# Experts summed in one TensorE bank, and attention divided on channel partitions

## The chip, the cores and the metric

The kernel runs on one core of one Trainium2 chip. The metric is the device time of one execution in microseconds. A profile records one such execution: what each engine did and when, what it waited for, and every DMA.

## The reference

The input is `x`, float32, 4 images of 128 channels and 64 x 64 pixels. Two layers follow each other, everything in float32.

```python
# layer 0
x = x + conv_mamba(group_norm(x))
# layer 1, on tokens t = (4, 4096, 128)
t = t + attention(ln(t))        # 4 heads of 32, softmax over 4096 keys
t = t + moe(ln(t))              # 8 experts, the best 2 of each token
# moe:
probs = softmax(x @ router_w + router_b)
top_p, top_i = top_k(probs, 2)
top_p = top_p / top_p.sum(-1)
expert_out = einsum("bnd,edc->bnec", x, expert_w) + expert_b
return einsum("bnk,bnkc->bnc", top_p, gathered(expert_out, top_i))
```

`conv_mamba` is a depthwise 3 x 3 convolution with norms and a GELU, then a state-space scan: the 128 channels form 4 groups of 32, which the same weights expand to 64 inner channels each, with 16 states for each inner channel, a recurrence over all 4096 pixels, and a gated output projection.

## The kernel before

**Blocks and units.** An image is cut into 8 blocks of 512 pixels. A block of the scan is 2 halves (`p`) of 16 states (`n`), so there are 4 x 8 x 2 x 16 = 1,024 units (b, i, p, n). The main loop issues one unit in each slot. `queued` ties every instruction of an engine to the one before it, so that each engine runs in the order in which the loop issues; DMAs, on SP's queue, are among them. Nearly all instructions are recorded by this one helper, which is why the profile gives line L445 to them; they are told apart by the names of their tiles.

**One slot.** (1) `flush` issues the stores that `send` has collected. (2) `fetched` asks for the `rows` (512 KB, B and C rows of the scan spread over 128 partitions) of the unit three slots ahead. `until` must first see that this unit's `inputs` task is done; while it is not, `until` makes catch-up passes, which advance the two lanes and do nothing else. (3) `decayed` computes `da` for the next unit (ScalarE Exp). (4) An attention group: 4 score matmuls `sc`, 2 Exps `pT` of 128 x 1024. (5) `scan`: VectorE multiplies `h<-rows,du`, scans, and multiplies `hc<-rows,h`. (6) TensorE adds `hc` into the bank `y` with an identity matmul; for images after the first, GpSimd first adds each pair of `hc`, which halves these matmuls. (7) The 4 `av` matmuls of the attention group of the slot before (`weighted`). The lanes advance at fixed places between these.

**Lanes.** Two queues of tasks, X and Y, each written as a generator that yields between stages; a lane advances two stages in a slot. Each lane has one PSUM bank (`work("X")`, `work("Y")`) and four rotating SBUF tiles (`tmp`). Y takes group norms, `first_norm`, `conv` and `inputs` (which also uses bank X for two short matmuls); X takes `closed` (end of layer 0 for a block: output projection `wout`, norms, q, k, v), `divided` and `finished` (the rest of layer 1 for a block). After the last unit both lanes take `finished`.

**Attention.** Keys are taken in 4 parts of 1,024, queries in 4 parts, 4 heads. `weighted` leaves a head's sums and its softmax denominator in `avs`, channels on partitions, and stores them to DRAM. `divided` reads the 4 heads back (`avl`), turns them with TensorE, and multiplies by the reciprocal on VectorE into `ao`, tokens on partitions. `finished` turns `ao` back into `aT`, applies the output projection, normalises and routes.

**Experts.** For each of 4 tiles of 128 tokens and each half of the experts, one matmul (two passes of TensorE, as each full float32 matmul here) computes 4 experts for 128 tokens into the lane's bank, and then VectorE folds them one by one:

```python
vector.scalar_tensor_tensor(
    acc[:, j, :], ps[:, e, :], pr[:, j, k : k + 1], acc[:, j, :],
    ALU.mult, ALU.add,
)
```

These stages are marked `"short"`, and a lane in them may advance four stages in a slot. At the end `acc` is turned with TensorE and joined with the expert biases in one bank, copied to `res` and stored.

The general path behind `tc.If` does not run with these inputs.

Of the kernel before, what the change touches and what calls it, by code (L numbers as in the profile page):

```python
# [13 lines left out]
ALU = mybir.AluOpType  # L14
# [22 lines left out]
def conv_mamba_attn_moe_kernel(ctx: ExitStack, tc: tile.TileContext, t: dict):  # L37
# [488 lines left out]

    group_of, y0_of, xn_of, pairs_of, in_of, gated, kqv = {}, {}, {}, {}, {}, {}, {}
# [147 lines left out]
    def inputs(b, i, p):  # L675

        xn, pairs = xn_of[b, i], pairs_of[b, i]
        r = slice(DI * p, DI * p + DI)
        ps = work("Y")
# [15 lines left out]
        bc = mix.tile([DI, BLK], F32, name="bc")  # L695
# [65 lines left out]
    def closed(b, i):  # L761
# [20 lines left out]
        summed(ps, [(wout[:, p, :], gated.pop((b, i, p))) for p in range(2)])  # L782
# [29 lines left out]
        split = []  # L812
        for d, w, bias in ((kd, wkn, bkn), (qd, wqn, bqn)):
            ps = work("X")
            mm(ps, w, xa)
            yield
            full = side.tile([P, BLK], F32, name="full")
            scalar.activation(full, ps, AF.Identity, bias=bias)
            hi = side.tile([P, BLK], F32R, name="hi", bufs=2)
            scalar.activation(hi, ps, AF.Identity, bias=bias)  # L820
            yield

            split.append((d, full, hi))
            lower(split.pop(), sj)
# [9 lines left out]

    def lower(what, s):
        d, full, hi = what
        lo = side.tile([P, BLK], F32R, name="lo", bufs=2)
        vector.tensor_sub(lo, full, hi.bitcast(F32))
        for half, w in enumerate((hi, lo)):
            w = w.bitcast(F32)  # L840
            if len(d.shape) == 4:
                send(d[:, :, half, s], w[:, None, :].to_broadcast([P, 2, BLK]))
            else:
                send(d[:, half, s], w)
# [96 lines left out]
    sums, partial, ao_of = [None], {}, {}  # L941

    def weighted(group):
# [10 lines left out]
        if last:  # L954
            avs = att.tile([P, BLK], F32, name="avs", bufs=2)
            scalar.copy(avs, av)
            if prev is not None:
                gpsimd.tensor_add(avs, avs, prev)

            d = dram.tile([P, BLK], F32, name=f"avd{q}{h}")  # L960
            send(d, avs)
            partial[b, q, h] = d
            if final and h == NH - 1:
                lanes["X"].append((("div", b, q), divided(b, q), []))
                for u in range(2):
                    i = 2 * q + u
                    lanes["X"].append((
                        ("out", b, i), lambda lane, b=b, i=i: finished(b, i, lane),
                        [("div", b, q)],
                    ))  # L970

    def divided(b, q):

        ao = att.tile([P, 2, NT, NH, DH], F32, name="ao", bufs=2)
        ao_of[b, q] = ao

        def load(h):
            w = att.tile([P, BLK], F32, name="avl", bufs=2)
            sync.dma_start(out=w, in_=partial.pop((b, q, h)))
            return w  # L980

        ahead = load(0)
        yield
        yield
        for h in range(NH):
            now = ahead
            if h + 1 < NH:
                ahead = load(h + 1)
            ps = transposed("X", by_tile(now))
            yield  # L990
            ps = ps.rearrange("p (j u d) -> p u j d", u=2, d=2 * DH)
            rden = small.tile([P, 2, NT, 1], F32, name="rden")
            vector.reciprocal(rden, ps[:, :, :, DH : DH + 1])
            vector.tensor_mul(
                ao[:, :, :, h, :], ps[:, :, :, 0:DH], rden.to_broadcast([P, 2, NT, DH])
            )
            yield

    def finished(b, qb, lane):

        ao = ao_of[b, qb // 2][:, qb % 2]
        td = kqv[b][3]
        s = slice(qb * BLK, (qb + 1) * BLK)
        acc = side.tile([P, NT, C], F32, name="acc", bufs=2)
        sync.dma_start(out=acc.rearrange("p j c -> p (j c)"), in_=td[:, s])
        ps = transposed(lane, ao.rearrange("p j h d -> p j (h d)"))
        yield
        aT = tmp(lane, "aT")
        scalar.copy(aT, ps)
# [32 lines left out]
        vector.tensor_reduce(m, pr, AX.X, ALU.add)  # L1042
        vector.reciprocal(m, m)
        vector.tensor_mul(pr, pr, m.to_broadcast(wide))
# [22 lines left out]
        ewf = ew.rearrange("p e c -> p (e c)")  # L1067
        for j in range(NT):
            for u in range(2):
                ps = work(lane, [P, NE // 2, C])  # L1070
                mm(
                    ps.rearrange("p e c -> p (e c)"), xf[:, j * P : (j + 1) * P],
                    ewf[:, u * BLK : (u + 1) * BLK],
                )
                yield "short"
                for e in range(NE // 2):
                    k = NE // 2 * u + e
                    vector.scalar_tensor_tensor(
                        acc[:, j, :], ps[:, e, :], pr[:, j, k : k + 1], acc[:, j, :],
                        ALU.mult, ALU.add,  # L1080
                    )
                yield "short" if k < NE - 1 or j < NT - 1 else None
# [6 lines left out]
        scalar.copy(prT, ps[0:NE, :])  # L1089
        yield  # L1090
        ps = work(lane)
# [253 lines left out]
```

## Time and profile before

| | |
|---|---|
| Median of 3 runs | 5860.53 us (5855.43 to 5865.17) |
| Profiled execution | 5853.82 us |
| Its span, first to last instruction | 5852.1 us |
| Mean granted TensorE clock | 0.94 |
| TensorE / VectorE / ScalarE / GpSimd busy | 87% / 72% / 68% / 35% |
| DMA: bytes, mean rate | 1030 MB, 176 GB/s |

In a line of a group, the first numbers after the bar are the time in which at least one instruction of the group ran and the mean length of one in ns; after the second bar comes the idle time of the engine before them and what ended it. A line of a stretch gives for each engine its busy time and its instructions, then the granted TensorE clock, the share of the time in which the DMA engines were busy, and their rate. A line of waits gives the waiting engine and tile, what it waited for, the sum in us, the number of waits and the longest.

### The profile page before, as it was taken

Reading aid. Unit: us, or ns where it says so; the run is one execution under the profiler, and the core shown is the slowest. Engines: PE = TensorE matmul, PEld = TensorE weight load, DVE = VectorE, ACT = ScalarE, POOL = GpSimd, SP = SyncE. Lnnn points to the kernel's source line nnn. Section 1 sums busy time; section 2 is a strip of 40 time slices with the busy share of each in tenths; the row PEclk is TensorE's granted clock in tenths of the full one; section 3 lists DMA queues with packets and bytes.
Section 4 is the critical chain, followed back from the end, with each engine's and each line's share of the span. In section 5 each row is a group of like instructions: output and inputs, shape, how many; then the busy total and the mean of one; then the engine's idle time right before and its main releaser. Section 6 shows DMA issues by size and latency. Waiting matters only on the chain. (4 is left out here: it accounts for less than half of the span.)

```text
span 5852.1 us, 61426 instructions
## 1 busy us (share of the span) xinstructions
PE 5075.6 (87%) x18378; PEld 2129.7 (36%) x18378; DVE 4221.9 (72%) x7155; ACT 3988.0 (68%) x6116; POOL 2033.6 (35%) x1821
## 2 busy tenths in 40 slices
PE   4676898988989898898999998898999998998896
PEld 2222343333333333333333333333333343343332
DVE  4888766778877787787888887888888888712222
ACT  3454676877767776777777776677877777665452
POOL 2333222335423443444443443444443434310000
PEclk8777999999999998999999999999999999999997
DMA  3455565556545555556555555457555555533211
GB/s 98 167 177 169 196 203 182 190 209 223 202 149 172 198 186 197 172 198 219 185 199 199 188 199 191 155 196 252 191 192 199 183 201 185 190 134 102 99 58 35
DMA packets 405509, 1030.33 MB, mean 176 GB/s; under 512 B 42785, under 2 KB 126130, under 8 KB 405170
## 3 DMA queue, kind: packets, MB, share of 16 engines
q1 hardware_dynamic: 404002, 1025.53, 51.5%
q8 instruction: 149, 2.44, 0.2%
q14 instruction: 190, 1.56, 0.1%
q10 hardware_dynamic: 1168, 0.80, 0.1%
HBM read 875.11 MB, written 134.22 MB: 172 GB/s over the span
## 5 line engine op out<-in xcount | busy, mean ns | idle before, releaser
L445 ACT ACTIVATE pT<-sc 128x1024 f32<-128x1024 f32 x2048 | 1981.1, 1020 | 879.0 <-PE sc L445 875.5
L445 PE MATMUL av<-pT,v 128*64 128x512 f32 x8192 | 2012.4, 612 | 0.5 <-ACT avs L445 0.2
L445 DVE TENSOR_TENSOR_SCAN h<-da,state,h 128x512 f32<-128x512 f32 x896 | 1271.6, 1419 | 276.2 <-ACT da L445 191.5
L445 PE MATMUL sc<-qs,ks 128*128 128x512 f32 x4096 | 1326.7, 445 | 76.7 <-ACT pT L445 40.3
L445 POOL TENSOR_TENSOR hc<-hc 128x512 f32<-128x512 f32 x384 | 557.4, 1452 | 1541.4 <-DVE hc L445 1367.3
L445 PEld LDWEIGHTS sc<-qs,ks 128*128 128x128 f32 x4096 | 724.5, 193 | 663.0 <-issue 240.9
L445 PEld LDWEIGHTS av<-pT,v 128*64 128x64 f32 x8192 | 503.9, 138 | 1198.3 <-issue 1115.1
L445 DVE TENSOR_TENSOR hc<-rows,h 128x512 f32<-128x512 f32 x1024 | 828.2, 809 | 73.6 <-DVE h L445 2.3
L445 DVE TENSOR_TENSOR h<-rows,du 128x512 f32<-128x512 f32 x1024 | 821.7, 802 | 57.3 <-DMA rows<-bcd 30.9
L445 PE MATMUL y<-hc,ident 128*128 128x512 f32 x1280 | 734.3, 660 | 79.6 <-DVE hc L445 70.0
L445 ACT ACTIVATE da<-delta,amat 128x512 f32<-128x512 f32 x1024 | 749.7, 732 | 30.9 <-DVE h L445 28.7
L445 ACT COPY state<-h 128x1 f32<-128x1 f32 x896 | 176.8, 197 | 373.3 <-DVE h L445 373.0
L445 DVE SCALAR_TENSOR_TENSOR acc<-ps_X,prX,acc 128x128 f32<-128x128 f32 x864 | 301.8, 349 | 169.6 <-PE ps_X L445 145.3
L445 ACT ACT_TABLE_LOAD x318 | 408.0, 1283 | 20.0 <-PE ps_Y L445 15.3
L445 PE MATMUL ps_X<-w_ew,xf 128*128 128x512 f32 x432 | 257.2, 679 | 112.4 <-DVE acc L445 112.2
L445 PEld LDWEIGHTS y<-hc,ident 128*128 128x128 f32 x1280 | 248.7, 206 | 257.1 <-DVE hc L445 129.6
L445 DVE RECIPROCAL rden<-ps_X 128x8 f32<-128x8 f32 x64 | 13.0, 203 | 348.8 <-PE ps_X L445 348.6
L445 POOL TENSOR_SCALAR rsX<-mvX 128x4 f32<-128x4 f32 x92 | 48.3, 525 | 600.6 <-DVE mvX L445 593.6
L445 POOL TENSOR_SCALAR du<-e 128x512 f32<-128x512 f32 x64 | 129.3, 2020 | 322.3 <-ACT e L445 322.3
L445 POOL TENSOR_TENSOR avs<-avs,prev 128x512 f32<-128x512 f32 x64 | 94.6, 1478 | 420.4 <-ACT avs L445 345.8
L445 POOL TENSOR_SCALAR rsY<-mvY 128x4 f32<-128x4 f32 x100 | 54.9, 549 | 533.6 <-DVE mvY L445 532.0
L445 ACT ACTIVATE xt<-ps_Y,shiftY,rsY 128x128 f32<-128x128 f32 x380 | 143.5, 467 | 127.4 <-POOL shiftY L445 119.9
(244 smaller groups left out, 5052.1 us busy)
## 6 DMA issues: line engine op xcount, KB each, us to landing
rows<-bcd SPq DMA_DIRECT2D x1024, 512.0 KB, 4.9
ks<-kd SPq DMA_DIRECT2D x256, 512.0 KB, 6.3
qs<-qd SPq DMA_DIRECT2D x130, 512.0 KB, 5.6
v<-vd SPq DMA_DIRECT2D x256, 256.0 KB, 6.2
avd<-avs SPq DMA_DIRECT2D x128, 256.0 KB, 2.0
pairs<-xn SPq DMA_DIRECT2D x128, 128.5 KB, 2.4
qd<-hi SPq DMA_DIRECT2D x32, 512.0 KB, 5.6
qd<-lo SPq DMA_DIRECT2D x32, 512.0 KB, 5.9
```

The source lines that it names most:

```text
L445: return lambda *args, **kw: queued(op(*args, **kw))
```

## The change

- **Experts.** The routing weights of the 8 experts (`prT`, 8 x 512) are stored to DRAM, and each pair of rows is read back spread over all partitions (`share`, 512 KB). VectorE multiplies the normalised tokens `xf` by it, 128 x 1024 at once, and TensorE adds the products with the experts' weights, all eight, into the bank in which biases and the turned residual lie already. The softmax's own normalisation is dropped, since the two best are normalised again. The `"short"` stages go.
- **Exclusion.** Bank X is now occupied from the biases to the copy of `res`. The set `held` keeps `inputs` (which uses bank X) and this part of `finished` apart: each waits for the other, two stages at a time.
- **Division.** `weighted` stores the last sums into one DRAM tensor, sums and denominators apart. `inverted` reads the denominators 128 x 32, takes reciprocals and stores them; it is run in three steps 2, 4 and 6 slots later, outside the lanes. `finished` reads the sums as `aT`, channels on partitions, and the reciprocals spread over the channels as `inv`, and VectorE multiplies. `divided`, its turns and the copy of `aT` go.
- **Pairs.** The pairwise addition of `hc` on GpSimd starts at slot 128 (`ALONE`) instead of 256.
- **Output projection in `closed`.** Each half now writes only its 64 output partitions, instead of both adding over 128.
- **q and k.** ScalarE no longer writes `full`; VectorE takes `lo` from the bank. `bc` moves to a `tmp` tile.

```diff
@@ inputs
+        while held:
+            yield
+            yield
+        held.add("in")
...
+        held.clear()
-        bc = mix.tile([DI, BLK], F32, name="bc")
+        bc = tmp("Y", "bc")[0:DI, :]
@@ closed
-        summed(ps, [(wout[:, p, :], gated.pop((b, i, p))) for p in range(2)])
+        for p in range(2):
+            r = slice(DI * p, DI * p + DI)
+            mm(ps[r, :], wout[:, p, r], gated.pop((b, i, p)))
...
-            full = side.tile([P, BLK], F32, name="full")
-            scalar.activation(full, ps, AF.Identity, bias=bias)
...
+            vector.scalar_tensor_tensor(
+                lo, ps, bias, hi.bitcast(F32), ALU.add, ALU.subtract
+            )
@@ weighted
+            if not final:
+                partial[b, q, h] = dram.tile([P, BLK], F32, name=f"avd{q}{h}")
+                send(partial[b, q, h], avs)
+                return
+            if h == 0:
+                total[b, q] = dram.tile([2, 2, NH, DH, BLK], F32, name=f"total{q}")
+            d = total[b, q]
+            send(d[:, :, h].rearrange("u k r q -> (u k) r q"), avs)
+            if h == NH - 1:
+                work_left = inverted(b, q)
+                later.extend((slot + n, work_left) for n in (2, 4, 6))
+    def inverted(b, q):
+        den = small.tile([P, 2 * NH * BLK // P], F32, name="den", bufs=1)
+        n = den.shape[1]
+        for u in range(2):
+            sync.dma_start(
+                out=den[DI * u : DI * u + DI, :],
+                in_=total[b, q][u, 1, :, 0].rearrange("h (a n) -> h a n", n=n),
+            )
+        yield
+        vector.reciprocal(den, den)
+        inverse[b, q] = d = dram.tile([2, NH, BLK], F32, name="inverse")
+        send(d.rearrange("u h (a n) -> (u h a) n", n=n), den)
+        yield
+        for u in range(2):
+            lanes["X"].append((
+                ("out", b, 2 * q + u), lambda lane, i=2 * q + u: finished(b, i, lane), [],
+            ))
+        yield
@@ finished
-        ps = transposed(lane, ao.rearrange("p j h d -> p j (h d)"))
-        yield
-        aT = tmp(lane, "aT")
-        scalar.copy(aT, ps)
+        aT, inv = tmp(lane, "aT"), tmp(lane, "inv")
+        sync.dma_start(out=aT, in_=total[b, q][u, 0].rearrange("h d q -> (h d) q"))
+        sync.dma_start(
+            out=inv, in_=inverse[b, q][u][:, None, :].to_broadcast([NH, DH, BLK])
+        )
...
+        vector.tensor_mul(aT, aT, inv)
...
-        for j in range(NT):
-            for u in range(2):
-                ps = work(lane, [P, NE // 2, C])
-                mm(...xf[:, j * P : (j + 1) * P], ewf[:, u * BLK : (u + 1) * BLK])
-                yield "short"
-                for e in range(NE // 2):
-                    vector.scalar_tensor_tensor(...)
...
+        shares = dram.tile([NE, BLK], F32, name=f"shares{lane}")
+        send(shares, prT)
+        yield
+        while lane == "X" and held:
+            yield
+            yield
+        if lane == "X":
+            held.add("out")
+        def share(e):
+            if lane == "X":
+                w = side.tile([P, 2, BLK], F32, name="share", bufs=3)
+            else:
+                w = mix.tile([P, 2, BLK], F32, tag="rows", name="share", bufs=4)
+            sync.dma_start(
+                out=w.rearrange("p k q -> p (k q)"),
+                in_=shares[e : e + 2].rearrange("e q -> (e q)")[None].to_broadcast([P, 2 * BLK]),
+            )
+            return w
...
+        ahead = deque(share(e) for e in (0, 2))
+        yield
+        yield
+        for e in range(0, NE, 2):
+            if e + 4 < NE:
+                ahead.append(share(e + 4))
+            yield
+            w = ahead.popleft()
+            vector.tensor_mul(w, w, xf[:, None, :].to_broadcast([P, 2, BLK]))
+            yield
+            for u in range(2):
+                mm(ps, ew[:, e + u, :], w[:, u, :], False, e + u == NE - 1)
+        yield
+        if lane == "X":
+            held.clear()
@@ main loop
+    ALONE = NB // 2 * 2 * NST
-            if b == 0:
+            if slot < ALONE:
...
+        while later and later[0][0] <= slot:
+            next(later.popleft()[1])
```

## The prediction

> **What bounds the kernel now.** I read the busy shares first. They are averages, so the second view is the busy time by stretch; its cuts are where the issue slots fall, found by counting the 1,024 `h<-rows,du` multiplies, one for each slot: slots 128 to 255, slots 256 to 1023, the attention that is left after the last slot with a scan, and the end after the last attention group.
>
> ```profile
> PE 5075.6 (87%) x18378; PEld 2129.7 (36%) x18378; DVE 4221.9 (72%) x7155; ACT 3988.0 (68%) x6116; POOL 2033.6 (35%) x1821
> ```
>
> ```profile
> core 0: us, PE busy (x) PEld busy (x) DVE busy (x) ACT busy (x) POOL busy (x), PEclk, DMA share, GB/s
> 576.80:1178.50 601.70, 553.43 (x1920) 227.69 (x1920) 425.73 (x607) 438.51 (x667) 166.28 (x154) 0.96 0.57 195
> 1178.50:5123.80 3945.30, 3534.89 (x13222) 1494.23 (x13221) 3199.90 (x5248) 2930.08 (x4515) 1648.81 (x1413) 0.96 0.57 193
> 5123.80:5747.30 623.50, 573.78 (x2326) 242.72 (x2324) 133.48 (x488) 344.42 (x410) 39.92 (x55) 0.99 0.29 97
> 5747.30:5852.10 104.80, 58.05 (x142) 26.34 (x140) 35.96 (x134) 10.80 (x21) 3.40 (x8) 0.58 0.06 21
> ```
>
> TensorE is busy 92%, 90% and 92% of the first three stretches; VectorE comes next with 71%, 81% and 21%. So from slot 128 on TensorE's work and its idle time make the length, and I keep the account on TensorE. The fourth stretch is a chain of latencies at a clock of 0.58. Third, what TensorE waits for:
>
> ```profile
> PE ps_X L445 <- DVE acc L445: 136.5, 99, 8.3
> PE ps_X L445 <- DMA avl<-avd: 49.7, 17, 8.2
> ```
>
> The first is the experts' loop: with one bank per lane, the next expert matmul waits until VectorE has folded the last one into `acc`. The second is the division's reload of its sums. The change takes both out. Fourth, the groups that it touches:
>
> ```profile
> L445 PE MATMUL av<-pT,v 128*64 128x512 f32 x8192 | 2012.4, 612 | 0.5 <-ACT avs L445 0.2
> L445 PE MATMUL y<-hc,ident 128*128 128x512 f32 x1280 | 734.3, 660 | 79.6 <-DVE hc L445 70.0 <-POOL hc L445 9.2
> L445 PE MATMUL ps_X<-w_ew,xf 128*128 128x512 f32 x432 | 257.2, 679 | 112.4 <-DVE acc L445 112.2 <-PE av L445 0.2
> L445 PE MATMUL ps_X<-zs,w_wout 128*128 128x512 f32 x128 | 63.4, 617 | 1.9 <-ACT zs L445 1.2 <-ACT state L445 0.7
> L445 PE MATMUL ps_X<-ident,avl 128*128 128x128 f32 x256 | 47.3, 314 | 62.8 <-DMA avl<-avd 49.7 <-DVE h L445 5.5 <-PE ps_X L445 1.6
> L445 DVE SCALAR_TENSOR_TENSOR acc<-ps_X,prX,acc 128x128 f32<-128x128 f32 x864 | 301.8, 349 | 169.6 <-PE ps_X L445 145.3
> ```
>
> I use busy time over count, because pipelined matmuls overlap: 0.574 us for a pass of `y`, 0.495 for `w_wout`, 0.246 for `av`, about 0.6 for an expert (two passes each; 307 us over 512 passes with lane Y's row).
>
> **What the Trainium skill says.** "TensorE: Matmul & The Clock Gate", Part 3 (row/col tiling), has matmuls whose outputs lie in different column groups run concurrently. The trace agrees: `av`, 64 columns to either half, has passes 2.0 times as dense as `w_wout`'s (0.246 against 0.495). "SBUF — State Buffer", Who interferes with whom: a VectorE instruction with two SBUF inputs contends with GpSimd instructions that read SBUF. The trace agrees: the 128x512 multiply `h<-rows,du` took 0.68 us at 1999.9 and 1.76 at 2005.7 beside GpSimd's `hc<-hc`. The new share multiplies are of that kind, the removed folds (one input in PSUM) are not. "DMA: Bandwidth & Descriptors", Why a DMA increments its semaphore by 16 and not by 1: a transfer is split over the largest number up to 16 that divides both sides' slowest dimension. No run here shows a transfer with a slowest dimension of 4.
>
> **The change, part by part.**
>
> *Pairs from slot 128.* 64 of the 640 `y` matmuls go: 128 passes at 0.574 = 73 us of TensorE, all in the first stretch. 64 GpSimd additions come, 1.45 us each (row `hc<-hc`) = 93 us, and VectorE slows beside them: `h` and `hc` average 0.79 us there and 0.81 in the second stretch, which pairs already, so two per slot add some 5 us; with waits for the port up to 64 x 1 us. TensorE would fall to 480 us of 602, VectorE rise to 430 to 490. The next limit is thus at hand: I take 50 of the 73 (0 to 73).
>
> *Output projection in two column halves.* 128 passes go from 0.495 to `av`'s 0.246: 32 us; taken 26 (16 to 32).
>
> *Division.* The 256 passes on `avl` (47.3) and the 128 on `ao` (some 22 with lane Y) go: 69 us of TensorE; taken 55 (35 to 69). Of the reload wait 45 us lie outside the end; I take 23 (0 to 45), since the first reader of the new aT can wait instead. For it come, in SP's queue ahead of later `rows` loads: sums to DRAM (as before), two small loads, one store, and per block one 256 KB load for aT and one for the inverse. There is room: `rows` is asked for three slots (15 us) ahead and lands in 4.9, and inversion is spread over three steps two slots apart. The 4x32x512 store, and the inverse's read with 4 in front, I expect on 4 of 16 engines: the page's DMA share 0.57 at 195 GB/s makes 21 GB/s an engine, so 64 KB each take an estimated 3.1 us. Hidden in the loop, and paid in the end.
>
> *Experts.* The passes stay 512, now four in a row instead of two: between the 0.495 of `w_wout` (four in a row) and 0.6, so 0 to -54; taken -25. VectorE gives up, per block of 512 tokens, 32 folds at 0.349 (11.2), three small softmax operations (0.6) and the division (1.3), and gets four 128x1024 multiplies, 1.2 clean (VectorE's 128x256 `ao` takes 0.424 and its 128x512 `tt` 0.686, so 0.26 more for each 256) to 1.6 beside GpSimd, and the aT multiply 0.7: 6.5 us less. ScalarE loses `full` (64 x 0.70) and the aT copy (32 x 0.59), 64 us. Neither is the bound, so both count zero; they are why I believe in part of the freed waits. Of the fold waits, 110 us lie outside the end (136.5 less 25.8): taken -55 (0 to -110). What can come instead: 128 share loads of 512 KB (67 MB, 6% of all bytes moved; DMA has 0.43 free), each asked for 1.5 slots before its multiply, while `rows`, of the same size, lands in 4.9 us, one slot. A late share stops the scan behind it on VectorE, and the fourth load waits on SP for a matmul. And `lo` now reads PSUM, so the next projection waits for VectorE too: 64 times up to 0.75. Together +25 (0 to 80).
>
> *The exclusion.* An output block now keeps bank X through the shares, so `inputs` waits on `held`, and the scan cannot go on without it: `until` then runs the two lanes with neither scan nor attention in between. Stepping through both slot loops gives 60 such catch-up passes before (36 in the prologue) and 113 after: 53 more, in 10 further places of some five, and 12 for 7 in two. The old ones can be priced: 6, 7, 7 and 3 passes lie in these stretches.
>
> ```profile
> 1005.50:1030.50 25.00, 13.47 (x34) 5.07 (x31) 3.38 (x4) 13.68 (x19) 7.03 (x5) 0.79 0.36 111
> 2333.90:2366.20 32.30, 24.54 (x64) 9.87 (x61) 12.57 (x49) 18.47 (x31) 11.90 (x14) 0.72 0.24 77
> 3646.70:3672.90 26.20, 17.42 (x56) 7.61 (x56) 5.12 (x13) 13.07 (x19) 4.02 (x6) 0.79 0.37 101
> 1834.50:1852.90 18.40, 14.70 (x52) 6.62 (x51) 5.85 (x17) 16.11 (x24) 10.29 (x10) 0.91 0.49 169
> ```
>
> TensorE's idle time in them is 31.8 us over 23 passes, 1.4 each; the work itself is only moved. 53 x 1.4 = +74. From below 1.1 a pass (+58), from above the whole stretch over four usual slots of 5 us, 3.6 a pass ((101.9 - 20) / 23, +189).
>
> *The end.* Two blocks run there, one per lane. Now the expert loop takes 53 us (5776 to 5829). The shares need a 2 us store, a 4.9 us load and 32 passes, 16 us at full clock and up to twice that at 0.58, about 25 to 40 us: -20 (0 to -35). The sums' way through DRAM takes store 4.3, load 2, store 2, load 4.3 against reload and transposes today, +4. Sum -16.
>
> **Sum.** -50 -26 -55 -23 -25 -55 +25 +74 -16 = -151. The profiled execution took 5853.8 us (span 5852.1); that gives 5703. The median of the runs shown is 6.7 above the profiled one, so I forecast 5710.
>
> **Rivals.** *Catch-up decides (slower).* Only one lane works in a catch-up pass, and its share multiplies wait there for loads asked for two passes before. At 3.6 us a pass (+189), new waits at 50 and no wait freed (-78 lost): -50 -26 -55 -25 -16 +189 +50 = +67, so 5928. It wins above 4.2 us a pass (225/53) with all gains there, above 2.8 without the freed waits. For it speaks that VectorE and TensorE both have long gaps in the four stretches; against it that 1.4 is measured. *Slots are set by the chain, not by TensorE.* In the second stretch TensorE still idles 410 us; if each slot's exp, scan and `av` hand over as today, only the first stretch (-25) and the last two (a quarter of the transposes -17, the folds' waits in the third stretch -35, end -16) gain, and +74 +25 take it back: +6, no change, about 5866. *The waits go altogether.* Folds -110, reload -45, passes -54, few new waits (+5): -50 -26 -55 -45 -54 -110 +5 +74 -16 = -277, so 5583. VectorE's lower load speaks for it, its 81% against it. That the change does not do what it says I leave out: the changed program holds the 128 wide multiplies and four expert passes in a row.
>
> **How the numbers follow.** About 0.2% (12 us) is what can be told from no change here. The forecast's own case, 5640 to 5790, has 0.5; the full gain 0.18; the chain 0.12, of which 0.08 end a little below (5790 to 5848), 0.03 within the 12 us and 0.01 above; catch-up 0.2. Faster 0.76, same 0.03, slower 0.21. The range 5570 to 5880 leaves most of the catch-up case and the far end of the full gain outside.
>
> **What would show it.** Right: `y` 128 passes fewer and the first stretch near 550 us; `w_wout` near 32 us busy; no `DVE acc` wait on TensorE; slots 256 to 1023 below 3900 us; catch-up places with 1 to 2 us of TensorE idle a pass. Wrong: VectorE waiting for `share` loads, or those places 15 us and more each.

## The result, and the profile after

The changed kernel takes **5898.69 us** (median of 4 runs, 5895.56 to 5900.8) against 5861.4 for the kernel before (4 runs): ratio 1.0064, interval 1.0047 to 1.0082. It is slower by 37 us, three times the 12 us that can be told from no change. The forecast was 5710.

The profiled execution has a span of 5893.7 us at a mean clock of 0.927. First the busy shares of the page after:

```profile
PE 5010.0 (85%) x17866; PEld 2078.3 (35%) x17866; DVE 4074.4 (69%) x6083; ACT 3927.9 (67%) x6018; POOL 2182.0 (37%) x1885
```

TensorE has 512 instructions fewer and was busy 66 us less; VectorE gave up 148 us, ScalarE 60. The work went away. The time didn't. The same four stretches as before show where (the columns are those of the prediction's table):

```profile
580.90:1173.30 592.40, 509.81 (x1794) 206.97 (x1794) 454.61 (x608) 433.64 (x660) 261.37 (x217) 0.93 0.58 197
1173.30:5219.20 4045.90, 3547.49 (x12997) 1482.56 (x12996) 3098.80 (x4507) 2889.21 (x4453) 1703.53 (x1418) 0.95 0.60 201
5219.20:5830.00 610.80, 561.42 (x2204) 230.82 (x2202) 71.85 (x224) 336.51 (x391) 38.27 (x51) 0.97 0.36 119
5830.00:5893.70 63.70, 35.52 (x100) 20.09 (x100) 21.46 (x67) 7.12 (x16) 3.40 (x8) 0.63 0.30 101
```

- Slots 128 to 255: -9 us. TensorE lost 44 us of work, GpSimd got 95, and the slots hardly noticed.
- Slots 256 to 1023: **+101 us**. TensorE's idle time rose from 410 to 498 us there, and its busy time did not fall (3535 to 3547).
- From slot 1024 on: 674.5 us against 728.3, -54 us. Of these, 41 lie in the last stretch (63.7 for 104.8), which the forecast had at -16. Two of the 32 output blocks have moved from here into the loop: by the plan (the order of issue, followed by stepping through the loop in the source) 24 are done before slot 1024, and 22 before the change.

What TensorE waits for, after:

```profile
PE ps_X L445 <- ACT xt L445: 122.4, 58, 8.9
...
PE sc L445 <- DMA ks<-kd: 68.6, 28, 6.3
...
PE ps_X L445 <- DVE aT L445: 57.9, 20, 7.5
...
PE ps_X L445 <- DVE lo L445: 37.9, 55, 2.5
```

The waits for `acc` and for `avl` are gone, as forecast. In their place stand a wait for `aT` (58 us, where the reload had 50), a wait for the keys twice as long (34.7 before), and a longer wait for `xt` (90.8 before). What VectorE waits for:

```profile
DVE den L445 <- DMA den<-total: 324.1, 3, 143.9
DVE h L445 <- ACT da L445: 316.7, 107, 18.7
DVE aT L445 <- DMA inv<-inverse: 197.6, 24, 24.1
...
DVE share L445 <- DMA share<-sharesX: 86.9, 23, 12.3
```

The first is harmless: three waits, all after the last slot with a scan, where VectorE has little else to do. The third may not be: each time VectorE stands for the inverse, the instructions behind it in its order stand too. Two of the groups that the change touches:

```profile
L445 PE MATMUL ps_X<-share,w_ew 128*128 128x512 f32 x448 | 233.0, 646 | 29.5 <-DVE share L445 29.4
L445 PE MATMUL ps_X<-zs,w_wout 128*64 128x512 f32 x128 | 34.1, 611 | 3.4 <-ACT state L445 2.2 <-ACT zs L445 1.2
```

The output projection has 34.1 us of busy time (forecast near 32) and expert passes take 0.52 us each (233.0 over 448) where 0.6 was before: of busy time, both steps came out.

The places of the catch-up passes are the second thing to see. The loop's plan has nine places of five or six passes each, 46 in all (the prediction spoke of ten), besides two with twelve; these are the stretches of the nine, each with the one slot in which they lie (three of the nine, and the sum line over all nine):

```profile
1487.60:1507.90 20.30, 17.10 (x53) 6.99 (x52) 7.31 (x15) 13.20 (x19) 3.84 (x3) 0.96 0.43 132
1836.70:1857.00 20.30, 14.63 (x53) 5.52 (x52) 7.48 (x22) 17.31 (x26) 6.89 (x5) 0.94 0.47 137
...
3188.80:3209.10 20.30, 14.66 (x54) 5.55 (x52) 7.89 (x22) 17.31 (x26) 6.85 (x5) 0.93 0.58 176
...
sum 187.60, PE 148.60 PEld 60.62 DVE 66.55 ACT 130.47 POOL 42.59; mean PE 16.51 PEld 6.74 DVE 7.39 ACT 14.50 POOL 4.73
```

Nine slots take 187.6 us, where the same nine took 54.3 in the kernel before, which makes passes in one of them alone. In the first of these stretches VectorE's timeline reads (start, length, instruction, idle time before it):

```profile
1491.49 1.22 DVE L445 TENSOR_TENSOR share<-share,xf 128x1024 f32<-128x1024 f32 x1
1504.15 0.69 DVE L445 TENSOR_TENSOR aT<-aT,inv 128x512 f32<-128x512 f32 x1 [11.44 <-DMA inv<-inverse]
```

and SP's, that the load it waited for was issued at 1498.41 only:

```profile
1497.93 0.43 SPq L445 DMA_DIRECT2D aT<-total  x1
1498.41 0.56 SPq L445 DMA_DIRECT2D inv<-inverse  x1
```

In catch-up passes one `out` task (`finished`) ends and the next begins at once. It asks for its inverse 5.7 us before VectorE multiplies by it.

**How long transfers take.** The page of before has a last column with the median time from issue to landing:

```profile
ks<-kd SPq DMA_DIRECT2D x256, 512.0 KB, 6.3
...
avd<-avs SPq DMA_DIRECT2D x128, 256.0 KB, 2.0
```

The page after leaves that column empty, so I took the times from the increments that each transfer leaves on its semaphore in the trace. A wide transfer leaves 16. The sums' store `total<-avs`, the denominators' load and the inverse's load leave 5: one each from 4 engines, and one more for the rest. The Trainium skill, "DMA: Bandwidth & Descriptors", Why a DMA increments its semaphore by 16 and not by 1, says that the sequencer posts the increments of unused engines at once; the trace agrees with 4 engines, as the prediction expected. What 4 engines cost is shown by the medians in us, the last column from a kernel told of below:

| 256 KB unless noted | before | after | all made wide (e_spread) |
|---|---|---|---|
| store of the sums, `avd<-avs` / `total<-avs` | 2.0 | 7.0 | 2.1 |
| load of the inverse (wide: each of four) | - | 8.95 | 2.2 |
| the same, from the first request to the last landing | - | 8.95 | 5.2 |
| `acc<-td`, asked for right behind the inverse | 6.0 | 8.8 | 2.9 |
| `prev<-avd` | 5.7 | 6.6 | 5.6 |
| keys, 512 KB, the slowest tenth above | 7.4 | 8.5 | 7.8 |

The row of `acc` has to be read with care: with eight loads ahead of it instead of two, the wide kernel asks for it later. Counted from the first load of the task, `acc` is there after 10.7 us in the changed kernel and after 9.3 in the wide one.

A landing time leaves out how long SP stands before it issues. SP issues DMAs in the order of the loop, so while it waits for a store to land, the loads behind it are not asked for. Its waits for the sums' store, in the changed kernel and then in e_spread:

```profile
SPq L445 <- DMA total<-avs: 72.9, 35, 5.7
```

```profile
SPq L445 <- DMA total<-avs: 3.7, 5, 1.6
```

In the kernel before, SP stood 0.7 us in all for `avd<-avs`.

### The profile page after: what moved, and what is told of

Read it like the earlier page. It is cut to its first block, busy times and chain, and to the rows that moved or that the text cites. A ratio compares the mean times of both kernels' runs of the same rounds, so it can differ in the third digit from the quotient of the medians.

```text
span 5893.7 us, 59603 instructions
## 1 busy us (share of the span) xinstructions
PE 5010.0 (85%) x17866; PEld 2078.3 (35%) x17866; DVE 4074.4 (69%) x6083; ACT 3927.9 (67%) x6018; POOL 2182.0 (37%) x1885
## 4 chain that ended last, share of the span: by engine, by line
PE 37%; DVE 21%; ACT 15%; DMA 9%; issue 8%; POOL 8%; SPq 1%; DVEq 0%; ACTq 0%; POOLq 0%
PE av L445 13%; DVE h L445 10%; PE sc L445 8%; PE ps_X L445 8%; ACT pT L445 5%; PE ps_Y L445 4%; DVE hc L445 3%; PE y L445 3%; ACT L445 3%; DVE cm L445 2%; ACT xt L445 2%; POOL du L445 2%; DMA ks<-kd 2%; DMA inv<-inverse 2%; POOL rsY L445 1%
## 5 line engine op out<-in xcount | busy, mean ns | idle before, releaser
L445 PE MATMUL av<-pT,v 128*64 128x512 f32 x8192 | 2042.2, 620 | 1.6 <-ACT avs L445 1.6
L445 DVE TENSOR_TENSOR_SCAN h<-da,state,h 128x512 f32<-128x512 f32 x896 | 1295.9, 1446 | 352.0 <-ACT da L445 269.9
L445 PE MATMUL sc<-qs,ks 128*128 128x512 f32 x4096 | 1322.3, 444 | 140.3 <-DMA ks<-kd 68.6
L445 POOL TENSOR_TENSOR hc<-hc 128x512 f32<-128x512 f32 x448 | 681.9, 1524 | 1619.9 <-DVE hc L445 1562.7
L445 DVE TENSOR_TENSOR h<-rows,du 128x512 f32<-128x512 f32 x1024 | 863.6, 843 | 70.2 <-DMA rows<-bcd 40.8
L445 PE MATMUL y<-hc,ident 128*128 128x512 f32 x1152 | 668.6, 667 | 105.3 <-DVE hc L445 67.9
L445 PEld LDWEIGHTS y<-hc,ident 128*128 128x128 f32 x1152 | 225.3, 209 | 266.5 <-DVE hc L445 125.2
L445 PE MATMUL ps_X<-share,w_ew 128*128 128x512 f32 x448 | 233.0, 646 | 29.5 <-DVE share L445 29.4
L445 DVE TENSOR_TENSOR share<-share,xf 128x1024 f32<-128x1024 f32 x128 | 158.7, 1254 | 143.4 <-DMA share<-sharesX 86.9
L445 DVE TENSOR_TENSOR_SCAN h<-da,h 128x512 f32<-128x512 f32 x128 | 179.6, 1403 | 57.8 <-ACT da L445 46.8
```

Source lines behind the costliest of these rows:

```text
L445: return lambda *args, **kw: queued(op(*args, **kw))
```

## The experiments

A kernel's distance is given to the changed kernel's 5899 unless another is named; each ran beside the kernel before on the same chip (5853 to 5861 us), and as that one was some 6 us slower in the changed kernel's own round, gains are smaller by that much when taken from the ratios. The expectations name theories by letters: E, the exclusion makes the loss; D, the division's way through DRAM; N, its narrow transfers; O, the place of the multiply in VectorE's order; P, the places of the `out` tasks. C is the hand-over between engines in experiments 1 to 4, and the catch-up passes later.

**1. Without the exclusion** (a_no_held). `inputs` works in bank Y alone:

```diff
-        while held:
...
-        pz = work("X")
+        pz = work("Y")
...
-        pb = work("X")
+        pb = work("Y")
```

> The changed kernel, but inputs uses bank Y alone (its four short matmuls follow each other there, still eight stages), so that nothing is held back; the shares, the division and all else stay. Catch-up passes fall from 113 to 75. Theory E (the exclusion makes the loss): slots 256 to 1023 lose most of the 101 us by which they grew, about 2.5 us a pass, so 5800 to 5820 us, and VectorE's long waits for inv in the catch-up places go with them. Theory D (the division's DRAM way makes it: VectorE waits in order for inv, 198 us in all): the waits stay and the time with them, 5880 to 5900. Theory C (slots are set by the hand-over between engines, and the loss is the two output blocks more that lie in slots 256 to 1023): no change, 5890 to 5900.

Measured: 6352.02 us, ratio 1.0852 (1.0829 to 1.0875), outside all three ranges. A miss of the experiment's own making: four matmuls now share one bank, and TensorE waits until ScalarE has emptied it (206.5 us on `zs`, 110.9 on `xin`). The exclusion isn't priced by it.

**2. Pairs from slot 256 again** (a_pairs_late).

```diff
-    ALONE = NB // 2 * 2 * NST
+    ALONE = NB * 2 * NST
```

> The changed kernel with the pairs added on GpSimd from slot 256, as before the change. 64 y matmuls come back in slots 128 to 255 (66 us of TensorE there), 64 GpSimd additions go. The stretch got 9 us shorter with the change; if TensorE's work set its length it should now become some 40 to 60 us longer (5945), if the hand-over sets it 0 to 10 us longer (5900 to 5908), and if GpSimd's additions cost VectorE what TensorE gains it stays (5899).

Measured: 5912.28, ratio 1.0101 (1.0084 to 1.0118): pairing from slot 128 is worth 14 us (22 by the ratios), not 50. The stretch of slots 128 to 255 grew by 14 us, between the ranges for a hand-over and for TensorE's work.

**3 and 4. The experts as before, with the new and with the old division** (a_old_experts, a_old_exp_div). The shares and `held` go out, the fold loop and its `"short"` stages come back:

```diff
-        ahead = deque(share(e) for e in (0, 2))
...
+        for j in range(NT):
+            for u in range(2):
+                mm(...xf[:, j * P : (j + 1) * P], ewf[:, u * BLK : (u + 1) * BLK])
+                yield "short"
+                for e in range(NE // 2):
+                    vector.scalar_tensor_tensor(acc[:, j, :], ps[:, e, :], ...)
```

The second also has `divided` and `ao` of before; what is left of the change in it are pairs, output projection, `lo` and `bc`.

> The changed kernel with the experts of before: folds on VectorE, the softmax's own sum, the short stages, no exclusion; division, pairs, output projection and lo as changed. Catch-up passes 67. Theory E: slots 256 to 1023 go back to about 3930 to 3960 us, the tail loses the some 40 us that it had gained, so 5830 to 5860. Theory D: the waits for inv stay and the freed work comes back, so 5900 to 5950. Theory C: the two blocks go back to the tail, about 5890.

> The changed kernel with both the experts and the division of before; only pairs from slot 128, the output projection in two column halves, lo from the bank and bc in a tmp tile remain. Catch-up passes 61. All theories: a little under before, 5820 to 5850. Against the kernel with the old experts alone it is the price of the division: theory D 50 us or more better, theory E within 20 us.

Measured: 5981.18 (ratio 1.0214, 1.0197 to 1.0231), above all three ranges, and 5833.64 (0.9964, 0.995 to 0.9978), as expected. So the new division cost **147 us** here, and the new experts took 82 off again. The rest of the change is worth 19.

**5. The same bytes, wide** (e_spread). The sums lie with the head in front, so that a head's store has 128 rows, and `aT` and the inverse come in four loads of 32 partitions:

```diff
-                total[b, q] = dram.tile([2, 2, NH, DH, BLK], F32, name=f"total{q}")
+                total[b, q] = dram.tile([NH, 2, 2, DH, BLK], F32, name=f"total{q}")
-            send(d[:, :, h].rearrange("u k r q -> (u k) r q"), avs)
+            send(d[h].rearrange("u k r q -> (u k r) q"), avs)
...
-        sync.dma_start(
-            out=inv, in_=inverse[b, q][u][:, None, :].to_broadcast([NH, DH, BLK])
-        )
+        for h in range(NH):
+            sync.dma_start(
+                out=inv[DH * h : DH * h + DH, :],
+                in_=inverse[b, q][u, h][None].to_broadcast([DH, BLK]),
+            )
```

> The changed kernel; the last sums are stored with one head's 128 rows in one piece, and aT and inv are read by four DMAs of 32 partitions each, so that no 256 KB transfer has a slowest dimension of 4. Six more DMAs per output block, 113 catch-up passes as in the changed kernel. Theory N (narrow transfers: the store took 7.0 us instead of 2.0, inv 9.0, and the DMAs behind them came late): VectorE's 198 us of waits for inv fall below 80, rows and ks land as before, and the time falls by 60 to 120 us to 5780 to 5840. Theory O (the place of the multiply in VectorE's order, whatever the landing): 10 to 30 us less. Theory E (exclusion): 5890 to 5900.

Measured: 5822.19, ratio 0.9942 (0.9921 to 0.9962): **76 us less**, with 192 DMAs more, in the range of theory N. But VectorE's wait for the inverse fell from 198 to 155 us only, not below 80 as that theory had it; TensorE's wait for the keys fell too (68.6 to 42.3), and SP's for the store.

**6. The multiply by the inverse on GpSimd** (e_pool).

```diff
-        vector.tensor_mul(aT, aT, inv)
+        gpsimd.tensor_mul(aT, aT, inv)
```

> The changed kernel with the multiply aT x inv on GpSimd instead of VectorE, so that the scan does not stand behind a wait for inv; transfers as they were. Theory O: most of the loss of slots 256 to 1023 comes back, 5800 to 5840. Theory N: VectorE is free, but rows, ks and acc still come late behind the narrow transfers and the output block waits as before: 20 to 40 us less, 5860 to 5880. Theory E: no change. GpSimd's own order (1.5 us more per block, its sums behind it) could make it 10 us worse.

Measured: 5924.85, ratio 1.0122 (1.0106 to 1.0139), 26 us more. This is outside every range, theory O's above all. The wait only moved: TensorE now waits 133.3 us for GpSimd's `aT`. To free VectorE brought no gain here, while the inverse came late for TensorE too.

**7. Out tasks kept off the middle of the cycle** (e_prio). The plan has 69 passes instead of 113.

```diff
-        while lane == "X" and held:
+        while lane == "X" and (held or (slot < len(units) and 18 <= slot % 32 <= 24)):
```

> The changed kernel, but an output block also leaves bank X alone in slots 18 to 24 of each 32, before the inputs task that has only five slots of room; the exclusion itself stays. Catch-up passes 69 instead of 113 (60 before the change), no other edit. Theory E: 44 passes at 1.4 to 3.6 us come back, 60 to 160 us, so 5740 to 5840. Theories N and O: the division's waits stay; at most the 1.1 us of idle TensorE a pass, 5850 to 5890.

Measured: 5856.79, ratio 1.0001 (0.9992 to 1.0009), 42 us less for 44 passes fewer: in the range of theories N and O, and below the 60 that theory E asked for at least.

**8. The old division with the new experts** (a_old_division). For room it loads shares one ahead, and has single buffers for `hi` and `lo`; its plan has 118 passes.

```diff
-        aT, inv = tmp(lane, "aT"), tmp(lane, "inv")
...
+        ps = transposed(lane, ao.rearrange("p j h d -> p j (h d)"))
...
-        ahead = deque(share(e) for e in (0, 2))
+        flush()
+        ahead = deque(share(e) for e in (0,))
```

> The changed kernel with the division of before (reload, turns on TensorE, ao) and everything else as changed; to make room share has two buffers instead of three (one load ahead instead of two) and hi and lo one. Catch-up passes 118, since the division's ten stages stand in lane X again. Theories N and O: the new division cost 147 us with the old experts, so 5750 to 5790 here, in spite of the passes. Theory E: 5880 to 5920, as the passes are as many. In between, both count.

Measured: 5942.8, ratio 1.0159 (1.0142 to 1.0176), above every range: 44 us more where experiment 4 had said 147 less. The two disagree, so the price of a division isn't a constant: something else changes with it. What that could be, the plan told: without the stages of `divided` ahead of them, `out` tasks start in other slots.

**9 to 12. Which transfer, both cures together, and the wide division with the old experts.** s_store makes only the store (and `aT`) wide, s_inv only the inverse's load; e_spread_prio is 5 and 7 together; s_old_exp is a_old_experts with the edit of 5. No edit is new.

> Only the 64 stores of the sums (and the loads of aT that follow from their new layout) move on all engines; the 32 reads of the inverse stay on 4. Theory N, every narrow transfer keeps 4 of the engines busy and delays the loads behind it, each in proportion to its count: 64 of 96 such transfers, so some two thirds of the 76 us, 5850 (5835 to 5865), with ks and prev landing nearly as early as before and the wait of VectorE for the inverse unchanged near 200 us. Rival W, the cost is VectorE's wait for the late inverse alone: 5885 to 5900.

> Only the 32 reads of the inverse move on all engines (four of 32 partitions each); the 64 stores of the sums stay on 4. Theory N: a third of the 76 us, 5874 (5860 to 5885). Rival W, the cost is VectorE's wait for the late inverse alone: nearly all of the 76 us, 5825 to 5840, with that wait down by a half or more.

> Both one-sided changes together: the sums and the inverse move on all engines (e_spread, 76 us below the changed kernel), and the out tasks keep off bank X in slots 18 to 24 of every 32 (e_prio, 42 us below it, 44 catch-up passes fewer). Theory N+C, the narrow transfers and the catch-up passes are two separate costs: the gains add up, 5899 - 76 - 42 = 5781, range 5765 to 5800. Rival I, both are the same cost: the passes are dear only because an out task that begins there asks for its inverse 5.5 us before it multiplies and VectorE stands for 11 to 13 us, which a quick inverse ends as well; then little is left for the second change, 5805 to 5830.

> The experts as before the change (no shares, no bank held), and the new division with its sums and inverse moved on all engines. With narrow transfers this kernel took 5981, with the old division 5834: the division cost 147 us there. Theory N, the 147 are the narrow transfers: they go nearly all, 5840 to 5865. Rival D, a part of the new division costs whatever its width (the round trip through DRAM, the reciprocals on VectorE, the catch-up passes, of which there are 67 against 61): only about the 76 us of e_spread come back, 5895 to 5915.

Measured: s_store 5837.38 (ratio 0.9968, 0.9956 to 0.998), -61; s_inv 5880.82 (1.0039, 1.0026 to 1.0053), -18; together 79, e_spread 76. So 64 stores cost 1.0 us each and 32 loads of the inverse 0.6. The wait of VectorE decides nothing by itself: ahead of the multiply it does not fall in s_store (144 us for the inverse and 59 more for `aT`, `acc` and `rows`, 203 in all for 198), it falls to 150 in s_inv, and s_store gains three times as much. SP's wait for the store goes with the gain: 6.3 us in s_store, 68.4 in s_inv. e_spread_prio takes 5762.57 (0.9837, 0.9823 to 0.985), 136 less, where the sum of the two single gains is 118: the two costs are separate, and together the cures bring rather more. s_old_exp takes 5906.53 (1.0087, 1.0073 to 1.0101): of the 147 us, 75 were the width, as rival D said, and 72 stayed open.

**13. Old experts, wide division, and out tasks where they were** (x_p8). Eight empty stages stand ahead of a pair of `out` tasks, no work is added:

```diff
+        def empty():
+            for _ in range(8):
+                yield
+
+        lanes["X"].append((("div", b, q), empty(), []))
         for u in range(2):
             lanes["X"].append((
-                ("out", b, 2 * q + u), lambda lane, i=2 * q + u: finished(b, i, lane), [],
+                ("out", b, 2 * q + u), lambda lane, i=2 * q + u: finished(b, i, lane),
+                [("div", b, q)],
             ))
```

> s_old_exp (5907) with one edit: eight empty stages of bank X stand ahead of each pair of out tasks, where the old division's ten stages stood; out tasks then start at slots 305, 336, 371 and 562, 593, 628 of the plan, against 305, 335, 368 and 562, 592, 626 with the old division, and 301, 317, 345 and 557, 573, 601 without the edit; catch-up passes 57 against 67. No work is added or taken away. Theory P, the missing 72 us are the place of the out tasks in the cycle of 32 slots: most of them come back, 5835 to 5865. Rival D, they are the new division's own price (round trip through DRAM, the wait of VectorE for the inverse, a TensorE clock that is lower by 0.01): 5890 to 5910 for ten passes fewer at 1 us each.

Measured: 5787.19, ratio 0.9873 (0.9855 to 0.989): **119 us below s_old_exp**, more than the open 72. The stretch of slots 256 to 1023 in s_old_exp, and then in x_p8:

```profile
1171.30:5215.80 4044.50, 3553.69 (x12999) 1487.44 (x12998) 3228.75 (x5251) 2906.07 (x4454) 1646.60 (x1418) 0.95 0.56 189
```

```profile
1176.50:5069.40 3892.90, 3486.33 (x12917) 1455.73 (x12916) 3177.39 (x5136) 2897.49 (x4443) 1660.63 (x1414) 0.96 0.59 196
```

152 us shorter, with some 80 TensorE instructions moved to the end. Plan and trace together show part of how: s_old_exp has 32 slots here in which lane X advances four stages instead of two (the `"short"` stages), x_p8 has 2. Those without a catch-up pass behind them, 30, take 7.7 us each, against 5.3 for a slot with two stages in each lane: an estimate of some 70 us. Ten catch-up passes fewer (57 for 67) come to it; the rest is not told apart. Nor do these slots alone explain the 72 us, since a_old_exp_div, with the old division, has 25 of them.

**14. Old division, new experts, out tasks kept off the middle** (a_old_div_prio): experiment 8 with the edit of 7.

> The old division with the new experts (a_old_division, 5943), and the out tasks kept off bank X in slots 18 to 24 of every 32: 73 catch-up passes against 118. The counterpart is e_spread_prio (5763), which has the new division with wide transfers. Theory C, the old division of a_old_division was dear only by its catch-up passes and by the places where they fell: 45 passes fewer and regular places, 5825 to 5870, that is some 60 to 100 over e_spread_prio for 65 us of transposes and the longer end. Rival S, it is the shares loaded a single one ahead and the single hi and lo buffers that this kernel needs for room (VectorE waits for a share 133 us there, 87 in the changed kernel): 5890 to 5915.

Measured: 5845.61, ratio 0.9982 (0.9975 to 0.9989), 97 less than a_old_division. In regular places the old division is thus 11 us better than the narrow new one (e_prio) and 83 worse than the wide one (e_spread_prio). Most of the disagreement of 4 and 8 was the places; what its shares loaded a single one ahead cost this kernel isn't told apart.

**15 and 16. The changed kernel with ten empty stages, and that with wide transfers** (y_n10, y_s10). The edit is x_p8's with `range(10)`; y_s10 adds that of e_spread.

> The changed kernel (5899) with ten empty stages of bank X ahead of each pair of out tasks; nothing else. Out tasks then start at slots 306, 335, 370 and 563, 592, 626 of the plan, against 301, 317, 343 and 558, 573, 599; catch-up passes 79 against 113. Theory P, the changed kernel is slower than the one before because its out tasks crowd into one part of the cycle and into catch-up places: the gain is between that of e_prio (42) and that of x_p8 (119), 5800 to 5850, so faster than before with its narrow transfers still there. Rival N, the narrow transfers decide: as with e_prio or less, 5855 to 5880.

> y_n10 with the sums and the inverse moved on all engines. The two costs add up as in e_spread_prio (-76 and more): theory P 5730 to 5775, below e_spread_prio (5763) by the better places of the first tasks of a pair; rival, the places of e_spread_prio are as good (8 more passes here, a later end): 5760 to 5785.

Measured: y_n10 5810.56, ratio 0.992 (0.9904 to 0.9936), **88 us less** with the narrow transfers still in. y_s10 **5732.42**, ratio 0.9789 (0.9775 to 0.9804), another 78 less, and the quickest of all: 2.1% below the kernel before. Their stretches from slot 256 on, y_n10 and then y_s10:

```profile
1173.40:5132.30 3958.90, 3503.14 (x12942) 1463.92 (x12942) 3077.62 (x4474) 2884.31 (x4445) 1720.13 (x1414) 0.96 0.61 205
5132.30:5807.40 675.10, 602.91 (x2358) 258.01 (x2356) 105.33 (x324) 346.91 (x416) 43.97 (x63) 0.94 0.37 122
```

```profile
1180.60:5103.70 3923.10, 3500.30 (x12943) 1460.85 (x12942) 3085.52 (x4474) 2883.91 (x4446) 1723.98 (x1414) 0.96 0.61 207
5103.70:5736.60 632.90, 592.91 (x2358) 253.92 (x2356) 106.25 (x324) 346.88 (x416) 43.85 (x63) 0.96 0.38 130
```

y_n10 wins in the loop alone (3958.9 against 4045.9). Half of that is TensorE idle time (498 to 456 us), half its busy time (3547 to 3503), at a clock of 0.96 instead of 0.95. Wide transfers bring 36 us in the loop and 42 behind it; of these 42, only 5 lie behind the last attention group. Three of the nine places, now, in y_n10:

```profile
1487.70:1492.40 4.70, 4.70 (x13) 1.06 (x13) 4.49 (x5) 2.35 (x5) 2.89 (x2) 0.82 0.33 106
1812.10:1816.80 4.70, 4.70 (x22) 2.26 (x22) 4.49 (x4) 2.32 (x5) 2.92 (x2) 1.00 0.27 92
1972.50:1978.30 5.80, 5.42 (x22) 1.64 (x20) 5.59 (x6) 5.25 (x9) 2.87 (x2) 1.00 0.80 250
```

An ordinary slot each, where the changed kernel had 20 us; one of the nine still holds three passes and takes 15.4. In all y_n10's plan has 79 passes, 113 in the changed kernel, so places and number of passes change together here.

## Why the prediction was wrong

The kernels form a chain from the one before to the changed one, and the steps of the prediction can be laid beside its links:

| step | forecast | measured | how |
|---|---|---|---|
| pairs, output projection, `lo` | -50 -26 = -76 | -19 | a_old_exp_div against before |
| division (turns, reload, +4 in the end) | -55 -23 +4 = -74 | -46 | x_p8 against a_old_exp_div, wide, eight empty stages ahead |
| experts (passes, folds, new waits, -20 in the end) | -25 -55 +25 -20 = -75 | -55 | y_s10 against x_p8, with 22 passes more |
| transfers on 4 engines | 0 in the loop | +78 | y_n10 against y_s10 |
| catch-up passes and places | +74 | +88 | changed kernel against y_n10 |
| sum | -151 | +46 | |

Read them to some 10 us: the kernel before, measured again with each, had medians from 5852.9 to 5861.4 (by the ratios the last link is 84 and not 88), and the links interact, so another order would divide the sum otherwise. The division's link also takes away 23 slots with four stages, the experts' link carries 22 of the exclusion's passes, and the last link holds 34 of the 53. The granted clock differs along the chain too: 0.939 in a_old_exp_div, 0.934 in x_p8, 0.938 in y_s10, 0.934 in y_n10, 0.926 in the changed kernel (means of their executions). Of the four executions of x_p8 the shortest (5771 us) has 0.938 and the longest (5794) 0.931, so a part of a link may be the clock's, as cause or as effect; no run separates them.

- **The step that failed by itself is "Hidden in the loop, and paid in the end".** The prediction had the 4 engines right, and put a store and a load at 4.3 us each, in the end alone. Measured were 7.0 and 8.95, and the cost is not hidden: of the 71 us between the profiled executions of y_n10 and y_s10, 36 lie in slots 256 to 1023, 37 in the attention behind them, 5 in the end, and -7 in the first 256 slots. By the medians it is 78 us, where 0 stood. The room for them was argued from the median of `rows`, 4.9 us. For `rows` it held in the main: the slowest tenth went from 7.4 to 8.5 us, against 15 us of lead, and VectorE waited 40.8 us for them instead of 30.9. But TensorE's wait for the keys doubled, and SP stood 73 us for the store. How these add up to the 78 is not shown.
- **"50 of the 73" for the pairs was far too much.** Undone alone they are worth 14 to 22. TensorE did lose its work in that stretch (44 us), and the slots stayed at 4.6 us each (4.7 before). The rival "Slots are set by the chain, not by TensorE" comes nearest here, though it too had -25 for this stretch, and -9 was measured; what sets these slots no run shows. The output projection's busy time fell as forecast, but the whole link is 19.
- **The exclusion: right in kind, the price low.** It was taken from TensorE's idle time in old places, 1.4 us a pass, "the work itself is only moved". In the nine places TensorE idles less than that, 0.85 us a pass (39 us over 46). Yet the moved work isn't given back in full. An estimate from the changed kernel's trace: a slot with two stages in each lane, and no pass before or behind it, takes 5.07 us in the mean (4.68 in the median), one with none 4.46 (3.62), so stages that ride along in a slot cost 0.6 to 1.1 us. Alone in a pass they cost 3.1 (187.6 less nine slots of 5.07, over 46). Net that is 2 to 2.5, so 53 passes are some +110 to +130, within the range given and below the 3.6 of the rival "Catch-up decides". y_n10 got 2.6 a pass (88 over 34) and e_prio 1.0 (42 over 44), each with the tasks in other places; why e_prio's passes were worth less isn't settled.
- **What the prediction didn't ask is where the `out` tasks go when `divided` ahead of them is gone.** It counted the stages that a removed task costs, and not that they had spaced the tasks behind. In the plan the first two outs of an image start at slots 301 and 317, against 304 and 333 before; ten empty stages put them at 306 and 335. In the kernel with the old experts the shift shows in the slots with four stages: 32 without empty stages, 2 with them. How the 88 us of y_n10 divide between fewer passes and better places stays open.
- **The freed waits: the names were right, the sum was not.** No wait for `acc` is left, but `aT` (58 us) took the reload's place, as the prediction allowed with "the first reader of the new aT can wait instead". VectorE waits 87 us for `shares` of lane X and 57 for those of lane Y; whether the prediction's 25 for all new waits was near the link of the experts (-55 for -75) doesn't tell, as it holds 22 passes too.
- **The end** was sized too low: the last stretch lost 41 us, for 16. The two blocks that moved into the loop are not what made the -54 from slot 1024 on: y_n10 has as many blocks left there as the kernel before, and takes 675.1 us for them.

Of the rivals, none describes the outcome. "Catch-up decides" has the sign, and catch-up as a part of it; its price didn't come, and that the sum went the same way owes as much to the transfers, which no rival had.

## What to carry to other kernels

Before a transfer is called hidden, count the engines that it runs on, and look at what is queued behind it and at what the queue itself will wait for: laying the same bytes out wide was worth 78 us. When a task goes out of an interleaved schedule, step through the plan for where the tasks behind it now start and how many catch-up passes come of it: ten empty stages, no work at all, were worth 88 us. Price work that leaves its slot by what it costs alone less what its slot gives back, and not by the idle time beside it.

## What the runs showed of the hardware

- A 256 KB store on 4 engines took 7.0 us, on 16 engines 2.1: 3.4 times (e_spread), where the forecast had 4.3 us. The broadcast load of the inverse, of the same size, took 8.95 on 4 engines; as four loads of 32 partitions each of them took 2.2, and the four together 5.2 from the first request to the last landing.
- With narrow transfers among them, the other loads of the queue land later: the slowest tenth of the keys' loads took more than 8.5 us, and more than 7.8 us with the same bytes moved wide (e_spread); in the kernel before it was 7.4.
- TensorE's work removed and its busy time are two things: the sum of its groups fell by 151 us from before to after, its busy time by 66, at a mean clock of 0.927 against 0.940. What sets that clock no run here tells.
